# Seven quarter products for the queries of fourteen head pairs, and a layernorm spread over seven heads

## The chip, the cores and the metric

The kernel runs on one core of one Trainium2 chip. The metric is the device time of one execution in microseconds; the time of a kernel is the median of its runs. Engines are named as in the profile: PE is TensorE (matmuls; PEld are its weight loads), DVE is VectorE, ACT is ScalarE, POOL is GpSimd, SP is SyncE, which here only issues transfers.

## The reference

One transformer block with adaptive layernorm: 2 batches of 1024 tokens, 256 channels, 16 heads of 128, all float32. Queries and keys get a bias and a rotary turn, the attention is causal, and a gated feed-forward part follows.

```python
h = _layernorm(x) * (1 + ca) + sa
q = (h @ Wq + bq) * scale; k = h @ Wk + bk; v = h @ Wv + bv   # per head: (n, 128)
q = q * cos + rotate_half(q) * sin                            # k alike
attn = softmax(where(causal, -max, q @ k.T))
x = x + ga * ((attn @ v) @ Wo + bo)
h = _layernorm(x) * (1 + cb) + sb
x = x + gb * ((silu(h @ Wgate) * (h @ Wup)) @ Wdown)
```

## The kernel before

The attention is cut into 32 units, one for each batch, group of two heads, and head: `units = [(b, g, h) ...]`, numbered `n`. Even `n` is the first head of its group (h = 0), odd `n` the second (h = 1). A unit runs eight steps `i`, one for each block of 128 queries. The whole program is written inside `tc.manual_schedule()`: each engine executes its instructions in the order in which the loop at lines 879 to 927 writes them.

In step `i` that loop writes, in this order:

- `shared_out` (L629, L632): one output projection of an older head on PE into the only bank of `ps_y`, and on DVE the sum `x += py * rden`. The next output projection can't start before this sum has read the bank.
- `score` (L542, L545): the product of query block i with the keys up to it, into one of two buffers of `ps_sc`, and on DVE the masked row minimum `nmax`.
- `turned` (L576, L588): the 32x32 turn of the probabilities of step i-1 on DVE; after steps 3 and 7 it issues 16 transfers on SP that put the blocks in place (`pT`).
- `expo` (L562): the exponential on ACT.
- `release`: what `project_qk` left over from the step before (see below).
- `project_qk` (L499 to L521) in steps 1, 3, 4 and 5: half the tokens (512) of the queries or keys of the next unit.
- `values` (L603, L611): probabilities times values of the unit before, in steps 0, 6 and 7.
- products of the values (`value_step`) in steps 0, 2 and 3, and `extras`: layernorm, weights of the feed-forward part, gates.

A projection of a query half is two matmuls into one bank of `ps_a` (two banks in all), one for each half of the 256 channels. ACT then adds the bias and swaps the halves of the head into `r1` (two instructions of 64 x 512, L511, reading the bank), POOL multiplies `r1` by the sine table (L512); in `release` of the next step DVE writes `dst = (pq + bias) * cos` (L515, reading the bank and the cosine table), and POOL adds `r1` to it (L518).

The values of groups 2 to 15 (counted over both batches, 14 groups) are not computed head by head. Both heads and both token halves of a group form a 2 x 2 product of quarters (tokens half by channel half, weights channel half by head), which `value_step` (L453 to L488) does with 7 quarter products in place of 8, in Winograd's way: `token_sum` makes four sums of token quarters once per batch (`tT`), `weight_sums` (L440) makes four sums of 128 x 128 weight quarters for each group on POOL, and the products are put together by two copies on ACT (`snap`), five additions on DVE that read a bank and a `snap`, and two additions on POOL. Steps 1 to 3 are in the second head of the group before, steps 4 to 7 in the group's own first head.

The layernorms between (of batch 1 before its attention, and of batch 0 before its feed-forward part) lie in `extras` (L792 to L812): statistics of the 8 token blocks (L224, L225) in units m-5 and m-4, a square root on ACT (L229) in m-4, scaling and a 32x32 turn of each block (L240, L273) in m-3 and m-2, with m = 14 and 30. The feed-forward weights are scaled on DVE (L318) in units 6, 7 and 8, in steps 2 and 5; `add_bias` (L398) adds a row to x on POOL in every step of units 17 and 20. `gate_rows("b")` issues two row broadcasts on SP in unit 7.

Of the kernel before, what the change touches and what calls it, by code (L numbers as in the profile page):

```python
# [11 lines left out]
F32 = mybir.dt.float32  # L12
I32 = mybir.dt.int32
AF = mybir.ActivationFunctionType
ALU = mybir.AluOpType
PSUM = bass.MemoryType.PSUM

P = 128
B, S, D = 2, 1024, 256
H, DH = 16, 128  # L20
HID = 704
NT = S // P
KC = D // P
HG = 2
# [3 lines left out]
QB = 512  # L28
# [9 lines left out]
def adaln_block(ctx: ExitStack, tc: tile.TileContext, a, cos_d, sin_d, out):  # L38
    nc = tc.nc
    pool = lambda name, bufs, **k: ctx.enter_context(tc.tile_pool(name=name, bufs=bufs, **k))  # L40

    const = pool("const", 1)
# [4 lines left out]
    ps_a = pool("ps_a", 2, space=PSUM)  # L47
# [14 lines left out]
    def load_x(b, t, n, eng):  # L62
        eng.dma_start(x[b][:, t : t + n, :], x_d[b, :, t : t + n, :])
# [19 lines left out]
    def warm_up(tiles):  # L83
# [22 lines left out]

    modT = const.tile([P, 4, KC, B], F32, name="modT")
    gate = {
        (n, b): const.tile([P, D], F32, name=f"g{n}{b}") for n in ("a", "b") for b in range(B)
    }  # L110
    bo_bc = const.tile([P, D], F32, name="bo_bc")
    bvacc = const.tile([P, D], F32, name="bvacc")
# [33 lines left out]

    def gate_rows(n):

        for b in range(B):
            row = grow_d["ab".index(n), b : b + 1, :]  # L150
            nc.sync.dma_start(gate[n, b], row.to_broadcast([P, D]))
# [51 lines left out]
    wpool = pool("w", 2)  # L203
# [182 lines left out]
    gbo = {}  # L386

    def bias_row():

        pb = ps_a.tile([P, 512], F32, tag="a", name="pbias")  # L390
        nc.tensor.matmul(pb[:, :D], ones, bvacc, start=True, stop=True)
        nc.vector.tensor_tensor(bo_bc, pb[:, :D], bo_bc, ALU.add)
        for b in range(B):
            gbo[b] = const.tile([P, D], F32, name=f"gbo{b}")
            nc.gpsimd.tensor_tensor(gbo[b], gate["a", b], bo_bc, ALU.mult)

    def add_bias(b, t):
# [39 lines left out]
        }[n]  # L437
        nc.gpsimd.tensor_tensor(tT[b, n], x0, x1, ALU.subtract)

    def weight_sums(b, g, n):  # L440

        w = weights[b, g]["v"]
        a11, a12, a21, a22 = (w[:, k, ts(h, DH)] for h in range(HG) for k in range(KC))
        if n == 0:
            s2 = tpool.tile([P, DH], F32, tag="ws", name=f"ws_{b}{g}")
            wsum[b, g] = (a21, s2, a11, a12)
            nc.gpsimd.tensor_tensor(a11, a11, a21, ALU.subtract)
            nc.gpsimd.tensor_tensor(s2, a22, a11, ALU.subtract)
        else:
            nc.gpsimd.tensor_tensor(a21, a21, a22, ALU.add)  # L450
            nc.gpsimd.tensor_tensor(a12, a12, wsum[b, g][1], ALU.subtract)

    def value_step(b, g, step):  # L453
        w = weights[b, g]["v"]
        quarter = lambda k, blk: hT[b, blk][:, k, :]
        if step == 1:
            vs[b, g] = vpool.tile([P, NT, HG * DH], F32, tag="v", name=f"v_{b}{g}")
            for n in (1, 2):
                snap[n] = tpool.tile([P, QB], F32, tag=f"s{n}", name=f"snap{n}_{b}{g}")
        part = lambda h, blk: vs[b, g][:, ts(blk, QB // P), ts(h, DH)]  # L460
        tiles = lambda t: t.rearrange("p (t d) -> p t d", d=DH)

        def product(tokens, wq):
            bank = ps_a.tile([P, 512], F32, tag="a", name=f"pv{step}_{b}{g}")
            for r in range(QB // P):
                nc.tensor.matmul(bank[:, ts(r, P)], tokens[:, ts(r, P)], wq, start=True, stop=True)  # L466
            return bank

        add = lambda eng, to, x0, x1: eng.tensor_tensor(to, x0, x1, ALU.add)  # L469
        if step == 1:  # L470
            nc.scalar.copy(snap[1], product(quarter(0, 0), w[:, 0, ts(0, DH)]))
        elif step == 2:
            bank = product(quarter(1, 0), w[:, 1, ts(0, DH)])
            add(nc.vector, part(0, 0), tiles(bank), tiles(snap[1]))
        elif step == 3:
            add(nc.vector, snap[1], product(tT[b, 2], wsum[b, g][1]), snap[1])
        elif step == 4:
            bank = product(quarter(1, 1), wsum[b, g][3])
            add(nc.vector, part(0, 1), tiles(bank), tiles(snap[1]))
        elif step == 5:  # L480
            nc.scalar.copy(snap[2], product(tT[b, 1], wsum[b, g][0]))  # L481
            add(nc.gpsimd, part(0, 1), part(0, 1), tiles(snap[2]))
        elif step == 6:
            add(nc.vector, snap[1], product(tT[b, 3], wsum[b, g][2]), snap[1])
            add(nc.gpsimd, part(1, 1), tiles(snap[1]), tiles(snap[2]))
        else:
            bank = product(tT[b, 4], w[:, 1, ts(1, DH)])
            add(nc.vector, part(1, 0), tiles(bank), tiles(snap[1]))  # L488

    def project_qk(u, s, n):  # L490

        b, g, h = u
        head = g * HG + h
        if n == 0:
            qks[u, s] = qkpool.tile([P, S], F32, tag=f"{s}T", name=f"{s}T_{b}{g}{h}")
        dst = qks[u, s]
        pq = ps_a.tile([P, 512], F32, tag="a", name=f"p{s}_{b}{g}{h}{n}")
        for k in range(KC):
            nc.tensor.matmul(  # L499
                pq,  # L500
                weights[b, g][s][:, k, ts(h, DH)],
                hT[b, n][:, k, :],
                start=(k == 0),
                stop=(k == KC - 1),
            )
        c = (R_BQ if s == "q" else R_BK) + head
        sl, half = ts(n, QB), DH // 2

        r1 = rot.tile([P, QB], F32, tag="r1", name=f"r1_{s}{b}{g}{h}{n}")
        for to, of in ((slice(0, half), slice(half, DH)), (slice(half, DH), slice(0, half))):  # L510
            nc.scalar.activation(r1[to], pq[of], AF.Identity, bias=cols[of, c : c + 1])  # L511
        nc.gpsimd.tensor_tensor(r1, r1, sin_t[:, sl], ALU.mult)  # L512

        def rest():
            nc.vector.scalar_tensor_tensor(  # L515
                dst[:, sl], pq, cols[:, c : c + 1], cos_t[:, sl], ALU.add, ALU.mult
            )
            nc.gpsimd.tensor_tensor(dst[:, sl], dst[:, sl], r1, ALU.add)  # L518


        held.append(rest)  # L521
# [234 lines left out]
    def extras(n, i):  # L756
# [8 lines left out]
            gate_b()  # L765
        if n == 6 and i == 3:
            gate_b_turn()
        if n == 7 and i == 3:
            gate_rows("b")

        if n in (2, 15) and i in (0, 1, 3):
            for m in {0: (1, 2), 1: (3,), 3: (4,)}[i]:
                token_sum(n // 15, m)
        if n > 2 and n % 2 and i in (0, 3) and n + 1 < N:
            weight_sums(*units[n + 1][:2], i // 3)

        if n == 2 and i == 7:
            ffn_scale_load()
        for m, name in ((5, "gate"), (6, "up"), (7, "last")):
            if n == m and i == 7:  # L780
                ffn_weight_load(name)
            if n == m + 1 and i in (2, 5):
                ffn_weight_scale(name, i // 4)
        if n in (3, 4, 8, 9) and i == 7:
            load_x(1, {3: 0, 4: 2, 8: 4, 9: 6}[n], 2, nc.scalar)
        if n == 29 and i == 7:
            ffn_down_load()
        if n == 31 and i in (1, 3, 5):
# [2 lines left out]

        for m, b, name in ((14, 1, "a"), (30, 0, "b")):  # L792

            j = i - 1 if n in (m - 5, m - 3) else i + 3
            if n in (m - 5, m - 4) and 1 <= i <= 4:
                ln_stats(b, name, j)
            if n == m - 4 and i == 6:
                ln_sqrt(b, name, 0, NT)
            if n in (m - 3, m - 2) and 2 <= i <= 5:
                ln_move(b, name, j - 1)  # L800
            if n in (m - 3, m - 2) and 1 <= i <= 4:
                ln_scale(b, name, j // 4, (j % 4,))
            if n in (m - 2, m - 1) and i == 6:
                ln_send(b, name, ((0, 1), (2, 3))[n - m + 2])
            if n == m and i in (4, 5, 7):
                blk = i // 6
                if i != 5:
                    dest = (new_hT if b else new_h2)(b, blk)
                else:
                    dest = (hT if b else h2s)[b, blk]  # L810
                for f in {4: (0,), 5: (1,), 7: (0, 1)}[i]:
                    ln_shift(b, name, blk, 0 if b else 2, dest, f)  # L812
# [4 lines left out]
        if n == 20:  # L817
            add_bias(1, i)

    filler = (0, 1, 3, 4, 5, 6)  # L820

    def shared_out(s, late=False):
# [3 lines left out]
    with tc.manual_schedule():  # L826
# [52 lines left out]
        for n, u in enumerate(units):  # L879
# [5 lines left out]
            for i in range(NT):  # L885
# [2 lines left out]
                if owed:  # L888
                    owed.pop()()
                ps, nmax = score(u, i)  # L890
                if n > 2 and h == 0 and i == 3:
                    value_step(b, g, 7)
                if i >= 1:
                    turned(u, i - 1)
                elif prev:
                    turned(prev, NT - 1)
                expo(u, i, ps, nmax)
                release()
                if i in (1, 3, 4, 5) and nxt:
                    project_qk(nxt, *{1: ("q", 0), 3: ("k", 0), 4: ("q", 1), 5: ("k", 1)}[i])  # L900
                if i in (6, 7) and prev:
                    values(prev, 1, 4 * (i - 6), 4 * (i - 5))

                if i in (0, 2):
                    if n in (1, 2):
# [1 line left out]
                            project_v(0, 1, 2 + 2 * n)  # L907
                    elif n == 0:
                        project_v(b, n, 4 + i, ps_o, "o")

                if n > 2 and (h == 0 or more) and i in (0, 2):
                    vg = (nb, ng) if h else (b, g)
                    for step in {(1, 0): (1, 2), (1, 2): (3,), (0, 0): (4, 5), (0, 2): (6,)}[h, i]:
                        value_step(*vg, step)
                if n == 0 and i in (6, 7):
                    project_v(0, 1, 2 * (i - 6))
                if not nxt and i in filler:
# [1 line left out]

                if prev and i == (0 if n > 2 else 2):  # L920
                    values(prev, 0, 0, 4)
                extras(n, i)
                if i == 7 and h == 1:
                    if more:
# [125 lines left out]
```

## Time and profile before

| | |
|---|---|
| median of 3 runs | 1061.25 us (1060.69 to 1061.36) |
| the profiled execution | 1061.52 us, of which the profile spans 1059.7 us |
| granted TensorE clock | 1.000 |
| busy: DVE, ACT, POOL | 701.0, 491.3, 468.5 us |
| transfers | 132.34 MB, 125 GB/s on average |

The share of busy time is over the whole span; a unit of the attention lasts 28.5 to 29.5 us in the middle of it, and in it PE's work follows without a gap. The span and what lies around it (1.82 us) make up the profiled execution's time.

### The profile page before, as it was taken

Reading aid. Unit: us, or ns where it says so; the run is one execution under the profiler, and the core shown is the slowest. Engines: PE = TensorE matmul, PEld = TensorE weight load, DVE = VectorE, ACT = ScalarE, POOL = GpSimd, SP = SyncE. Lnnn points to the kernel's source line nnn. Section 1 sums busy time; section 2 is a strip of 40 time slices with the busy share of each in tenths; the row PEclk is TensorE's granted clock in tenths of the full one; section 3 lists DMA queues with packets and bytes.
Section 4 is the critical chain, followed back from the end, with each engine's and each line's share of the span. In section 5 each row is a group of like instructions: output and inputs, shape, how many; then the busy total and the mean of one; then the engine's idle time right before and its main releaser. Section 6 shows DMA issues by size and latency. Waiting matters only on the chain.

```text
span 1059.7 us, 13263 instructions
## 1 busy us (share of the span) xinstructions
PE 1055.0 (100%) x3834; PEld 638.4 (60%) x3834; DVE 701.0 (66%) x1523; ACT 491.3 (46%) x930; POOL 468.5 (44%) x461
## 2 busy tenths in 40 slices
PE   9999999999999999999999999999999999999998
PEld 5655566566666665665666666666565666555747
DVE  5667776777777776766676666666777866545331
ACT  5644444454445454444554444454454554562110
POOL 5755464645353554855644544434444544200100
PEclk9999999999999999999999999999999999999999
DMA  5466646666565646565565656454555657423201
GB/s 191 91 173 161 155 112 153 148 148 150 125 157 117 147 112 155 112 152 120 117 148 113 147 113 152 107 144 97 144 112 128 144 132 171 107 59 71 70 0 40
DMA packets 68379, 132.34 MB, mean 125 GB/s; under 512 B 19366, under 2 KB 23476, under 8 KB 68308
## 3 DMA queue, kind: packets, MB, share of 16 engines
q1 hardware_dynamic: 66060, 126.17, 50.6%
q10 hardware_dynamic: 2168, 5.20, 1.5%
q8 instruction: 31, 0.51, 0.2%
q14 instruction: 40, 0.33, 0.1%
q0 software_dynamic: 80, 0.13, 0.1%
HBM read 25.52 MB, written 2.10 MB: 26 GB/s over the span
## 4 chain that ended last, share of the span: by engine, by line
PE 99%; DVE 0%; issue 0%; POOL 0%; POOLq 0%
PE po L603 23%; PE ps L542 23%; PE py L629 10%; PE pq L499 10%; PE pk L499 10%; PE pv L466 8%; PE pgu L658 7%; PE pd L716 2%; PE pv L411 1%; PE pd_0w L716 1%; PE pd_1w L716 1%; PE warm_ps L85 0%; PE ptx_a L254 0%; PE pd L705 0%; PE pm L122 0%; DVE wupT L318 0%
## 5 line engine op out<-in xcount | busy, mean ns | idle before, releaser
L562 ACT ACTIVATE p<-ps,nmax 128x128 f32<-128x128 f32 (+7 forms) x256 | 190.3, 743 | 353.9 <-DVE nmax L545 353.6
L542 PE MATMUL ps<-kT,qT 128*128 128x512 f32 (+3 forms) x768 | 289.6, 486 | 0.0
L603 PE MATMUL po<-pT,v 128*128 128x512 f32 (+3 forms) x768 | 263.7, 486 | 0.2 <-DMA pT<-t 0.2
L545 DVE CUSTOM_DVE_ANT_0 ps<-ps,mask 128x128 f32<-128x128 f32 (+7 forms) x256 | 195.1, 762 | 100.5 <-PE ps L542 100.1
L632 DVE SCALAR_TENSOR_TENSOR x<-py,rden,x 128x256 f32<-128x256 f32 x256 | 122.2, 479 | 179.7 <-PE py L629 176.3
L603 PEld LDWEIGHTS po<-pT,v 128*128 128x128 f32 x768 | 143.6, 190 | 122.5 <-issue 93.5
L576 DVE STREAM_TRANSPOSE t<-p 128x128 f32<-128x128 f32 (+7 forms) x256 | 197.9, 773 | 5.3 <-DMA pT<-t 3.0
L542 PEld LDWEIGHTS ps<-kT,qT 128*128 128x128 f32 x768 | 145.8, 190 | 77.4 <-issue 63.4
L512 POOL TENSOR_TENSOR r_q<-r_q,sin_t 128x512 f32<-128x512 f32 x64 | 82.4, 1287 | 162.4 <-ACT r_q L511 161.0
L629 PE MATMUL py<-wo,o 128*128 128x256 f32 x512 | 151.8, 381 | 0.3 <-DVE x L632 0.3
L629 PEld LDWEIGHTS py<-wo,o 128*128 128x128 f32 x512 | 90.0, 191 | 77.5 <-issue 49.1
L499 PE MATMUL pq<-hT,wq 128*128 128x512 f32 x256 | 120.5, 593 | 0.0
L499 PE MATMUL pk<-hT,wk 128*128 128x512 f32 x256 | 120.3, 592 | 0.0
L512 POOL TENSOR_TENSOR r_k<-r_k,sin_t 128x512 f32<-128x512 f32 x64 | 81.7, 1277 | 47.0 <-ACT r_k L511 46.8
L518 POOL TENSOR_TENSOR kT<-kT,r_k 128x512 f32<-128x512 f32 x64 | 81.2, 1269 | 42.2 <-DVE kT L515 36.4
L511 ACT ACTIVATE r_q<-pq,cols 64x512 f32<-64x512 f32 x128 | 87.6, 684 | 23.5 <-PE pq L499 19.9
L518 POOL TENSOR_TENSOR qT<-qT,r_q 128x512 f32<-128x512 f32 x64 | 81.8, 1278 | 27.1 <-DVE qT L515 24.6
L511 ACT ACTIVATE r_k<-pk,cols 64x512 f32<-64x512 f32 x128 | 87.6, 684 | 10.7 <-PE pk L499 7.0
L499 PEld LDWEIGHTS pk<-hT,wk 128*128 128x128 f32 x256 | 47.5, 190 | 41.4 <-issue 34.9
L499 PEld LDWEIGHTS pq<-hT,wq 128*128 128x128 f32 x256 | 46.1, 190 | 32.8 <-issue 30.3
L611 ACT COPY o<-po 128x512 f32<-128x512 f32 x64 | 37.3, 582 | 59.5 <-PE po L603 59.5
L469 POOL TENSOR_TENSOR v<-v,snap 128x512 f32<-128x512 f32 x14 | 17.7, 1265 | 93.2 <-ACT snap L481 93.2
(135 smaller groups left out, 967.5 us busy)
## 6 DMA issues: line engine op xcount, KB each, us to landing
pT<-t SPq DMA_DIRECT2D x512, 128.0 KB, 2.4
pT<-t SPq DMA_DIRECT2D x512, 64.0 KB, 2.0
wq<-in_Wq SPq DMA_DIRECT2D x16, 256.0 KB, 3.1
wk<-in_Wk SPq DMA_DIRECT2D x16, 256.0 KB, 4.1
wv<-in_Wv SPq DMA_DIRECT2D x16, 256.0 KB, 4.1
wo<-in_Wo SPq DMA_DIRECT2D x16, 256.0 KB, 3.0
out<-yo SPq DMA_DIRECT2D x15, 128.0 KB, 1.7
x<-in_x ACTq DMA_DIRECT2D x4, 256.0 KB, 3.1
```

Source lines behind the costliest of these rows:

```text
L466: nc.tensor.matmul(bank[:, ts(r, P)], tokens[:, ts(r, P)], wq, start=True, stop=True)
L499: nc.tensor.matmul(pq, weights[b, g][s][:, k, ts(h, DH)], hT[b, n][:, k, :], start=(k == 0), stop=(k == KC - 1),)
L511: nc.scalar.activation(r1[to], pq[of], AF.Identity, bias=cols[of, c : c + 1])
L512: nc.gpsimd.tensor_tensor(r1, r1, sin_t[:, sl], ALU.mult)
L518: nc.gpsimd.tensor_tensor(dst[:, sl], dst[:, sl], r1, ALU.add)
L542: nc.tensor.matmul(ps[:, c:e], qT[:, ts(i, P)], kT[:, c:e], start=True, stop=True)
L545: nc.vector.tensor_tensor_reduce(ps[:, :L], ps[:, :L], mask[:, NT - 1 - i :, :].rearrange("p t k -> p (t k)"), -SCALE, FLT_MAX, ALU.add, A ...
L562: nc.scalar.activation(p[:, :L], ps[:, :L], AF.Exp, bias=nmax, scale=-1.0, accum_out=dens[u][:, i : i + 1])
L576: nc.vector.transpose(t32[blk][:, :, j, : i + 1, :].rearrange("p c k b -> p k c b"), p[:, : (i + 1) * P].rearrange("p (k c a) -> p k c a", ...
L603: nc.tensor.matmul(po[:, off * P :], vs[b, g][:, k, ts(h, DH)], pT[:, off:, :, k, :], start=(k == 0), stop=(k == last),)
L629: nc.tensor.matmul(py[:, :D], outs[u][:, ts(t, P)], weights[b, g]["o"][:, h, :], start=True, stop=True)
L632: nc.vector.scalar_tensor_tensor(x[b][:, t, :], py[:, :D], rdens[u][:, t : t + 1], x[b][:, t, :], ALU.mult, ALU.add)
```

## The change

The queries of the same 14 groups are now made by the same 7 quarter products. `value_step` becomes `set_step(b, g, name, step)` and serves both; for the queries a product is one matmul with 512 columns in which the weight quarter is the stationary operand. The two heads' queries of the next group are made in the second head of a group (h = 1), the values of a group in its own first head (h = 0), one product in each of seven steps. `project_qk` is left for the keys (from unit 3 on), in steps 3 and 5 of h = 1 and in steps 2 and 5 of h = 0.

A finished quarter of the queries is in SBUF, no longer in a bank: `rotary` (which holds what followed the matmuls in `project_qk`) reads it there, and its last two operations write it in place. `rotary` is called from the list `due`, after the `values` of the same step. `weight_sums` makes the sums for queries too, in steps 0 and 1 of the same unit, in a new order.

```diff
-    def value_step(b, g, step):
-        w = weights[b, g]["v"]
+    due = []
+
+    def set_step(b, g, name, step):
+        w = weights[b, g][name]
...
+        if name == "q" and step in (1, 6):
+            h = step // 6
+            qks[(b, g, h), "q"] = qkpool.tile([P, S], F32, tag="qT", name=f"qT_{b}{g}{h}", bufs=3)
...
+                nc.tensor.matmul(bank, wq, tokens, start=True, stop=True)
             return bank
 
+        def done(h, blk):
+            if name == "q":
+                due.append(lambda: rotary((b, g, h), "q", blk, part(h, blk)))
...
         elif step == 2:
             bank = product(quarter(1, 0), w[:, 1, ts(0, DH)])
             add(nc.vector, part(0, 0), tiles(bank), tiles(snap[1]))
+            done(0, 0)
         elif step == 3:
-            add(nc.vector, snap[1], product(tT[b, 2], wsum[b, g][1]), snap[1])
+            nc.scalar.copy(snap[2], product(tT[b, 1], s1))
         elif step == 4:
-            bank = product(quarter(1, 1), wsum[b, g][3])
+            add(nc.vector, snap[1], product(tT[b, 2], s2), snap[1])
+        elif step == 5:
+            bank = product(quarter(1, 1), s4)
             add(nc.vector, part(0, 1), tiles(bank), tiles(snap[1]))
-        elif step == 5:
-            nc.scalar.copy(snap[2], product(tT[b, 1], wsum[b, g][0]))
             add(nc.gpsimd, part(0, 1), part(0, 1), tiles(snap[2]))
+            done(0, 1)
         elif step == 6:
-            add(nc.vector, snap[1], product(tT[b, 3], wsum[b, g][2]), snap[1])
+            add(nc.vector, snap[1], product(tT[b, 3], s3), snap[1])
             add(nc.gpsimd, part(1, 1), tiles(snap[1]), tiles(snap[2]))
+            done(1, 1)
         else:
             bank = product(tT[b, 4], w[:, 1, ts(1, DH)])
             add(nc.vector, part(1, 0), tiles(bank), tiles(snap[1]))
+            done(1, 0)
...
+    STEPS = (
+        {0: 1, 1: 2, 3: 3, 4: 4, 5: 5, 6: 6, 7: 7},
+        {0: 1, 1: 2, 2: 3, 4: 4, 5: 5, 6: 6, 7: 7},
+    )
...
-                if i in (1, 3, 4, 5) and nxt:
-                    project_qk(nxt, *{1: ("q", 0), 3: ("k", 0), 4: ("q", 1), 5: ("k", 1)}[i])
+                setted = n > 2 and (not h or more) and ((nb, ng, "q") if h else (b, g, "v"))
+                if setted and i in STEPS[h]:
+                    set_step(*setted, STEPS[h][i])
+                if n < 3:
+                    proj = {1: ("q", 0), 3: ("k", 0), 4: ("q", 1), 5: ("k", 1)}
+                else:
+                    proj = {3 if h else 2: ("k", 0), 5: ("k", 1)}
+                if i in proj and nxt:
+                    project_qk(nxt, *proj[i])
                 if i in (6, 7) and prev:
                     values(prev, 1, 4 * (i - 6), 4 * (i - 5))
+                while due:
+                    due.pop(0)()
```

The layernorms in `extras` take seven units: statistics of two blocks in each of units m-8 to m-5 (steps 1 and 2), the square root in m-5, and scaling and turn of three blocks in each of m-4 to m-2 (steps 1 to 4).

```diff
-            j = i - 1 if n in (m - 5, m - 3) else i + 3
-            if n in (m - 5, m - 4) and 1 <= i <= 4:
-                ln_stats(b, name, j)
-            if n == m - 4 and i == 6:
+            if m - 9 < n < m - 4 and i in (1, 2):
+                ln_stats(b, name, 2 * (n - m + 8) + i - 1)
+            if n == m - 5 and i == 3:
                 ln_sqrt(b, name, 0, NT)
-            if n in (m - 3, m - 2) and 2 <= i <= 5:
-                ln_move(b, name, j - 1)
-            if n in (m - 3, m - 2) and 1 <= i <= 4:
-                ln_scale(b, name, j // 4, (j % 4,))
+            t = 3 * (n - m + 4) + i - 1
+            if m - 4 <= n < m - 1 and 2 <= i <= 4 and t - 1 < NT:
+                ln_move(b, name, t - 1)
+            if m - 4 <= n < m - 1 and 1 <= i <= 3 and t < NT:
+                ln_scale(b, name, t // 4, (t % 4,))
```

To make room for a third query buffer, the two gate rows of the feed-forward part lie in a weight buffer and are loaded in unit 30 rather than in unit 7, the two rows of `gbo` overwrite `bvacc` and `bo_bc`, and two loads of x for batch 1 are issued a unit or two earlier.

## The prediction

> **What bounds the kernel now.** I read the page's busy shares first, then the chain that ended last, then the groups of PE by shape, and at the end the timelines of single units.
>
> ```profile
> PE 1055.0 (100%) x3834; PEld 638.4 (60%) x3834; DVE 701.0 (66%) x1523; ACT 491.3 (46%) x930; POOL 468.5 (44%) x461
> ...
> PE 99%; DVE 0%; issue 0%; POOL 0%; POOLq 0%
> ```
>
> PE works for 1055.0 of the 1059.7 us and makes up 99% of the chain. Its waits sum to 1.6 us: 1.1 at the start, 0.33 for a sum of L632 (unit 7) and 0.2 for a `pT` transfer. So each us of PE work that goes is a us of the end, as long as no other engine makes PE wait. How long an instruction holds PE is read from starts that follow each other, since the recorded lengths overlap:
>
> ```profile
> 160.39 1.88 PE L499 MATMUL pq<-hT,wq 128*128 128x512 f32 x4
> 162.11 0.59 PE L629 MATMUL py<-wo,o 128*128 128x256 f32 x2
> 162.54 0.81 PE L542 MATMUL ps<-kT,qT 128*128 128x384 f32 x2
> 163.19 1.05 PE L466 MATMUL pv<-ws,tT 128*128 128x128 f32 x8
> 164.08 0.60 PE L629 MATMUL py<-wo,o 128*128 128x256 f32 x2
> 164.51 1.02 PE L542 MATMUL ps<-kT,qT 128*128 128x512 f32 x2
> ```
>
> A matmul shows as two instructions. A query half (two matmuls of 512 columns) holds PE for 162.11 - 160.39 = 1.72 us; one 512-column score holds it 0.86 us (the next row starts at 165.37); a quarter product of the values, made of four 128-column matmuls, 0.89 us; an output projection 0.43 us.
>
> The engines behind PE, in a plain odd unit (5) and one with layernorm (11); columns are PE, PEld, DVE, ACT, POOL:
>
> ```profile
> 155.36:183.86 28.50, 28.50 (x105) 17.25 (x104) 19.66 (x44) 13.70 (x28) 11.79 (x12) 1.00 0.60 141
> 328.00:356.60 28.60, 28.60 (x105) 17.24 (x104) 22.42 (x53) 14.88 (x28) 11.84 (x12) 1.00 0.50 111
> ```
>
> DVE is the second: 19.66 of 28.50 us, before the change adds to it.
>
> **The change on PE.** Per group, 8 matmuls of 512 columns for the queries become 7: 4 x 1.72 = 6.88 us become 7 x 0.86 = 6.02 us. 14 x 0.86 = 12.0 us go. That a product which stands alone costs no more than half a pair is read from the single score above. The rest of PE's list keeps its instructions. Per unit the work moves little: an odd unit swaps three value products (2.67) and 3.44 of queries for 6.02, an even one four value products and 3.44 for seven (6.23); both come to about 28.5 us.
>
> **What is added elsewhere, 14 times each.** ACT: two copies of 128x512 at 0.58 (L471, L481), 16 us in all, and four rotary pairs (L511, 1.37 each) that now read SBUF. The only bound I have for another source is the ACT rows of this width, 0.58 to 0.78 us, so -0.1 to +0.1 each; ACT is busy for half a unit, which hides it. POOL: two additions at 1.27 to 1.32 (L469) and four weight sums at 0.455 (L447), 62 us in all. DVE: five additions at 0.60 from start to start (the L469 rows record 0.677), 42 us in all. An odd unit, which now holds all queries, goes on DVE from 19.66 by two more L515 (0.63 start to start) and three more additions to 22.7 us, and on POOL to 12 x 1.27 + 2 x 1.27 + 4 x 0.455 = 19.6 us, both of 28.4. On rates alone all of this hides under PE.
>
> **The new cost: a DVE turn with both operands in SBUF.** Before, L515 read a bank and the cosine table. A query quarter is now in SBUF, so 56 of the L515 read two SBUF operands. The trace has that form in L318, beside POOL's additions:
>
> ```profile
> 193.68 1.27 POOL L518 TENSOR_TENSOR qT<-qT,r_q 128x512 f32<-128x512 f32 x1
> 193.96 1.67 DVE L318 SCALAR_TENSOR_TENSOR wgateT<-raw,s_bc 128x640 f32<-128x640 int32 x1
> 194.91 1.85 POOL L469 TENSOR_TENSOR v<-snap,snap 128x512 f32<-128x512 f32 x1
> 204.02 0.81 DVE L318 SCALAR_TENSOR_TENSOR wgateT<-raw,s_bc 128x640 f32<-128x640 int32 x1
> 204.08 1.88 POOL L512 TENSOR_TENSOR r_q<-r_q,sin_t 128x512 f32<-128x512 f32 x1
> ```
>
> The same DVE instruction takes 0.81 us when it starts before POOL's, and 1.67 when POOL began 0.28 us earlier: it ends 0.7 us after POOL's does. The POOL instruction that comes second takes 1.85 or 1.88 in place of 1.27. So the later one waits for the other's whole instruction. A query turn costs 0.63 if it comes first, up to 0.63 + 1.27 if not.
>
> The Trainium skill speaks against the change here: "SBUF — State Buffer", section "Who interferes with whom", says that a DVE instruction with two SBUF inputs and a GpSimd one that reads SBUF exclude each other for a whole instruction. By it all 56 turns could lose up to a POOL instruction; the rows above agree, and the sum below doesn't rest on the page.
>
> Does that wait reach PE? The tight spot is `ps_y`'s only bank: output projection i+1 waits for DVE's sum of step i, which stands behind all DVE work of step i-1. Take t = 0 at the end of query product 2 (step 1 of an odd unit). PE: projection 0.43, score 1.08, product 3 1.94, projection 2.37, score 3.23, key half 4.95; then projection 4 wants the sum of step 3. DVE: addition until 0.8, sum 1.25, minimum (0.48) 1.75, turn of the probabilities (0.37) 2.1. ACT makes `r1` (1.38) from 0.8 to 2.2; then POOL's sine product (1.27) runs from 2.3 to 3.55, and DVE's query turn, which overwrites what ACT reads, is free at 2.2 too. If DVE comes first it ends at 2.85 and the sum of step 3 at 3.3: 1.65 us to spare. If POOL does, 4.2 and 4.65: 0.3 to spare. The last quarter (product 7, turned in step 0 of the next unit) leaves 0.9 us by the same count, or nothing where POOL is first, as it probably is, for DVE arrives 0.4 us after ACT is done.
>
> What eats these margins, with POOL first: unit 7, two blocks of statistics (0.5 each from start to start) and a weight scaling of 0.74 to 1.67, of which one block hides in the wait: 1.8 us. Units 6 and 8, the same in an even unit: 1.0 each. Units 11 and 27, scale and turn of two blocks (0.55 and 0.36 each): 0.6 each. Units 9, 23 and 25, statistics: 0.2 each. Unit 17, where POOL has eight `add_bias` of 0.73 more and ACT and DVE wait behind it: 0.8. The other groups 0.15 each, 2.0. Sum 8.4 us. With DVE first nearly all of it is covered: 0.5. The traced pairs give no rule for a tie; since POOL leads at the last quarter of every group and POOL's list is dense in step 6, I take two thirds, 5.5 us.
>
> **Edits that I cost at nothing.** The layernorms keep their instructions; spread, they take an even load from units 12, 13, 28 and 29 and put it in short steps, which is in the list above. The square root and its two table loads (1.28 each) move to unit 9, step 3; by the count above the exponential of step 4 then ends at 11.3, and score 6 wants its buffer at 12.0; uncovered, 2 us. The gate rows take 1.08 us of SP in unit 7 and lie in a gap (SP idle from 226.8 to 228.9 before the next 16 transfers); in unit 30 they are at the same step, and what queues behind them is the first half of `pT`; uncovered, 1.1 us once. `gbo` in place and the earlier loads of x keep their instructions.
>
> **The sum.** 1059.7 - 12.0 + 5.5 = 1053.2 of span, with the 1.82 us around it 1055.0; the profiled execution was 0.27 us above the median, so 1054.7 us.
>
> **The rivals.**
> 1. *All waits hide* (DVE first in most ties, or POOL's waits shorter): 0.5 us of stalls, 1061.25 - 12.0 + 0.5 = 1049.8. For it: PE waited 0.33 us in unit 7 before, although DVE there ran L318 for 1.67 us in the same step. Against it: the slots after products 2 and 3 are shorter now (step 1 of an odd unit 1.72 us of PE, before 2.58).
> 2. *DVE becomes the pacer of odd units*, which ends on the slower side. The query turn must wait not for one POOL instruction but for two in a row, since POOL has the next one ready. Half the turns at 2.54 and half at 1.27 make 22.7 + 7.6 = 30.3 us of DVE in a unit of 28.4: 1.9 x 14 = 26.6, 1075.8 us. It decides from 28.4 - 22.7 + 0.86 = 6.6 us of such waits per odd unit, 1.64 per turn; all four at two would give 63 us. For it: POOL's sine products and additions stand back to back in steps 5 and 6. Against it: in the two rows of 1.67 us DVE's wait was 0.86 us and the POOL instruction behind was held, so a waiting DVE is let in.
> 3. *The gain is eaten*: stalls between 9.9 and 14.1 us, the bound of 8.4 above plus what I cost at nothing; about 1061. For it: my count has no time for signals between engines (POOL starts L512 0.08 us after ACT's L511 ends).
> 4. *A lone product costs more than half a pair*: were it 0.05 us, 98 x 0.05 = 4.9 us less gain, 1059.6 with the forecast's stalls. Only the single score speaks, and against it.
>
> **How the numbers follow.** Forecast (1 to 9.9 us of stalls, rival 4 within it) 0.50; rival 1 0.27; rival 3 0.08; rival 2 0.15. The likeliest gives 1054.7, its own range 1050.2 to 1059.1. Reaching to rival 1 and over rival 3, and leaving out rival 2 and the tail below, the range is 1049.3 to 1063.0. No change means within 0.2% (2.1 us), about what a measurement can tell: rival 3 alone, 0.08; faster 0.77; slower 0.15.
>
> **What would show it.** Right: 98 lone query products, each holding PE 0.86 us; PE's busy time down by 12; L515 on queries in odd units at a mean between 0.7 and 2.0 us; PE's waits for L632 of 1 to 9 us, longest in unit 7. Wrong: waits of PE for anything but L632, such as a weight sum on POOL or a bank of `ps_a`; DVE above 28 us in plain odd units; or no waits at all.

## The result, and the profile after

The changed kernel takes 1066.66 us (median of 5 runs, 1065.90 to 1068.35), the kernel before 1061.36 us beside it (5 runs, 1060.69 to 1063.03). The ratio is 1.005, 95% interval 1.0035 to 1.0065: slower by 0.5%, where the forecast was 0.6% faster. The profiled execution took 1067.2 us and spans 1065.4 us, at a granted clock of 1.000.

The busy shares and the chain of the changed kernel:

```profile
PE 1050.1 (99%) x3806; PEld 633.1 (59%) x3806; DVE 779.6 (73%) x1593; ACT 505.8 (47%) x958; POOL 540.7 (51%) x545
...
PE 80%; DVE 13%; issue 2%; POOL 1%; DMA 1%; ACT 1%; SPq 1%; DVEq 0%; ACTq 0%; POOLq 0%
PE ps L579 20%; PE po L640 18%; PE py L666 9%; PE pk L529 8%; PE pgu L695 7%; PE pv L483 6%; PE pq L487 6%; DVE qT L552 4%; DVE t L613 2%; DVE ps L582 2%; PE pd L753 2%; DVE qT L494 1%; PE pq L529 1%; DVE x L669 1%; PE pv L416 1%
```

PE has the 28 matmul instructions less, yet only 80% of the chain is PE, where it was 99%: DVE is now 13% of it, with the query turn (L552) as its largest line. DVE's busy time rose by 78.6 us. PE's recorded busy time fell by 4.9 us only, though 12.0 us of work are gone from its list: a matmul that is held is recorded longer (0.70 us for 0.59 in the last row of the passage below), so about 7 us of what PE loses stand inside its busy time.

PE's waits (us in total, times, longest):

```profile
PE py L666 <- DVE x L669: 9.1, 17, 1.1
PE pv L483 <- DVE v L494: 1.3, 1, 1.3
PE warm_ps L85 <- POOL ones L79: 1.1, 1, 1.1
```

The wait is the one that the prediction named, for the sum that frees the bank of `ps_y`. The view counts a wait only past the recorded end of the instruction before, and records of matmuls overlap, so it understates the loss. I therefore took the gap between the starts of each two successive matmul instructions and subtracted the median gap of the width of the earlier one (0.429 us for 512 columns, 0.3225 for 384, 0.216 for 256, 0.112 for 128). What is left over, where it is more than 0.01 us and summed over the span ("stalls" from here on), is 6.4 us before and 24.1 us after. The change saves 12.0 us of PE and adds 17.7 us of stalls: +5.7, which is the difference of the spans (1065.4 - 1059.7). Stalls are always those of the one profiled execution, which can lie up to 2.5 us from the median of its kernel's runs.

That the saving is there is seen in unit 19, in PE's timeline (start, length):

```profile
576.69 1.02 PE L487 MATMUL pq<-tT,wsq 128*128 128x512 f32 x2
577.55 0.59 PE L666 MATMUL py<-wo,o 128*128 128x256 f32 x2
577.98 1.45 PE L579 MATMUL ps<-kT,qT 128*128 128x512 f32 x4
579.27 1.02 PE L487 MATMUL pq<-hT,wq 128*128 128x512 f32 x2
580.13 1.88 PE L529 MATMUL pk<-hT,wk 128*128 128x512 f32 x4
```

A lone product holds PE from 576.69 to 577.55, and another from 579.27 to 580.13: 0.86 us each, half a pair.

Units 19 (odd) and 20 (even), which have no layernorm and no weights of the feed-forward part (start and end; length; busy time of PE, PEld, DVE, ACT, POOL; clock; DMA share; GB/s):

```profile
565.27:593.67 28.40, 28.40 (x87) 15.66 (x86) 22.25 (x43) 15.70 (x31) 16.34 (x15) 1.00 0.62 148
593.67:622.78 29.11, 28.91 (x130) 19.38 (x129) 22.11 (x44) 12.85 (x27) 19.97 (x24) 1.00 0.49 109
```

No engine is near its limit: DVE works 22.25 of 28.40 us. A plain group takes 28.40 + 29.11 = 57.51 us where, by the starts of its scores, it took 28.50 + 29.39 = 57.89: of the 0.86 us that left PE's list 0.48 comes back, as one stall in the even unit.

The query turns and what stands before them (busy us, mean ns of one, idle before):

```profile
L552 DVE SCALAR_TENSOR_TENSOR qT<-qT,cols,cos_t 128x512 f32<-128x512 f32 x56 | 87.9, 1570 | 4.7 <-ACT r_q L548 4.3
L552 DVE SCALAR_TENSOR_TENSOR kT<-pk,cols,cos_t 128x512 f32<-128x512 f32 x64 | 45.4, 710 | 0.8 <-ACT r_k L548 0.8
L548 ACT ACTIVATE r_q<-qT,cols 64x512 f32<-64x512 f32 x112 | 80.6, 719 | 88.4 <-POOL qT L494 67.0
```

The same line takes 710 ns on keys, which it reads from a bank, and 1570 ns on queries, which it reads from SBUF. 87.9 - 56 x 0.71 = 48 us of DVE are waiting inside the instruction.

The place where PE pays, at the end of unit 19 and the start of unit 20 (the timeline, with rows left out; in brackets the idle time before and what ended it):

```profile
590.87 1.45 ACT L548 ACTIVATE r_q<-qT,cols 64x512 f32<-64x512 f32 x2 [4.46 <-POOL qT L494]
...
592.47 1.27 POOL L549 TENSOR_TENSOR r_q<-r_q,sin_t 128x512 f32<-128x512 f32 x1 [1.63 <-ACT r_q L548]
592.60 1.68 DVE L552 SCALAR_TENSOR_TENSOR qT<-qT,cols,cos_t 128x512 f32<-128x512 f32 x1
594.21 0.68 DVE L494 TENSOR_TENSOR qT<-pq,snapq 128x512 f32<-128x512 f32 x1
594.81 0.47 DVE L669 SCALAR_TENSOR_TENSOR x<-py,rden,x 128x256 f32<-128x256 f32 x1
594.98 1.45 ACT L548 ACTIVATE r_q<-qT,cols 64x512 f32<-64x512 f32 x2 [0.95 <-DVE qT L494]
595.41 1.23 DVE L613 STREAM_TRANSPOSE t<-p 128x1024 f32<-128x1024 f32 x1
596.51 1.27 POOL L549 TENSOR_TENSOR r_q<-r_q,sin_t 128x512 f32<-128x512 f32 x1 [0.81 <-ACT r_q L548]
596.57 1.76 DVE L552 SCALAR_TENSOR_TENSOR qT<-qT,cols,cos_t 128x512 f32<-128x512 f32 x1
598.52 0.48 DVE L669 SCALAR_TENSOR_TENSOR x<-py,rden,x 128x256 f32<-128x256 f32 x1
599.07 0.70 PE L666 MATMUL py<-wo,o 128*128 128x256 f32 x2 [0.20 <-DVE x L669]
```

Two quarters are turned in one passage. POOL multiplies product 6's quarter by the sine from 592.47; DVE's turn of the same quarter, which starts at 592.60, ends at 594.28, 0.54 us after POOL's instruction has. So DVE adds up product 7 only at 594.21, ACT reads the sum from 594.98, and now the second meeting comes: POOL at 596.51, DVE at 596.57, 1.76 us long. Behind it stands the sum of L669 (598.52), and behind that PE's projection at 599.07.

### The profile page after: what moved, and what is told of

It reads as the page before. It is cut to its first block, busy times and chain, and to the rows that moved or that the text cites. A ratio compares the mean times of both kernels' runs of the same rounds, so it can differ in the third digit from the quotient of the medians.

```text
span 1065.4 us, 13531 instructions
## 1 busy us (share of the span) xinstructions
PE 1050.1 (99%) x3806; PEld 633.1 (59%) x3806; DVE 779.6 (73%) x1593; ACT 505.8 (47%) x958; POOL 540.7 (51%) x545
## 4 chain that ended last, share of the span: by engine, by line
PE 80%; DVE 13%; issue 2%; POOL 1%; DMA 1%; ACT 1%; SPq 1%; DVEq 0%; ACTq 0%; POOLq 0%
PE ps L579 20%; PE po L640 18%; PE py L666 9%; PE pk L529 8%; PE pgu L695 7%; PE pv L483 6%; PE pq L487 6%; DVE qT L552 4%; DVE t L613 2%; DVE ps L582 2%; PE pd L753 2%; DVE qT L494 1%; PE pq L529 1%; DVE x L669 1%; PE pv L416 1%
## 5 line engine op out<-in xcount | busy, mean ns | idle before, releaser
L669 DVE SCALAR_TENSOR_TENSOR x<-py,rden,x 128x256 f32<-128x256 f32 x256 | 121.6, 476 | 113.9 <-PE py L666 108.7
L666 PE MATMUL py<-wo,o 128*128 128x256 f32 x512 | 154.5, 386 | 9.5 <-DVE x L669 9.1
L666 PEld LDWEIGHTS py<-wo,o 128*128 128x128 f32 x512 | 87.8, 190 | 86.1 <-issue 42.6
L548 ACT ACTIVATE r_q<-qT,cols 64x512 f32<-64x512 f32 x112 | 80.6, 719 | 88.4 <-POOL qT L494 67.0
L555 POOL TENSOR_TENSOR kT<-kT,r_k 128x512 f32<-128x512 f32 x64 | 86.6, 1353 | 29.0 <-DVE kT L552 27.5
L548 ACT ACTIVATE r_k<-pk,cols 64x512 f32<-64x512 f32 x128 | 87.3, 682 | 11.6 <-PE pk L529 8.1
L552 DVE SCALAR_TENSOR_TENSOR qT<-qT,cols,cos_t 128x512 f32<-128x512 f32 x56 | 87.9, 1570 | 4.7 <-ACT r_q L548 4.3
L290 POOL TENSOR_SCALAR h<-xt_b,modT 128x512 f32<-128x512 f32 x8 | 6.3, 798 | 96.6 <-DMA xt_b<-t 96.6
L483 PEld LDWEIGHTS pv<-wv,tT 128*128 128x128 f32 x336 | 44.0, 191 | 18.7 <-issue 13.4
```

What stands on the lines that cost most here:

```text
L552: nc.vector.scalar_tensor_tensor(dst[:, sl], pq, cols[:, c : c + 1], cos_t[:, sl], ALU.add, ALU.mult)
L666: nc.tensor.matmul(py[:, :D], outs[u][:, ts(t, P)], weights[b, g]["o"][:, h, :], start=True, stop=True)
L669: nc.vector.scalar_tensor_tensor(x[b][:, t, :], py[:, :D], rdens[u][:, t : t + 1], x[b][:, t, :], ALU.mult, ALU.add)
```

## The experiments

In the expectations, P is the theory that the query turn's meeting with POOL's sine product is the cause: both read SBUF, and the end of ACT's pair lets both go. N puts the time down to the layernorms spread over more units, W to DVE's added work, the five additions per group. The ratios are against the kernel before, run on the same chip; its median there was 1061.65 to 1062.37 us.

**1. The changed kernel with the old place of the layernorms** (e1). The lines of `extras` as they were:

```diff
-            if m - 9 < n < m - 4 and i in (1, 2):
-                ln_stats(b, name, 2 * (n - m + 8) + i - 1)
...
+            j = i - 1 if n in (m - 5, m - 3) else i + 3
+            if n in (m - 5, m - 4) and 1 <= i <= 4:
+                ln_stats(b, name, j)
...
```

> The queries by quarter products, with the layernorms as before the change (statistics in units m-5 and m-4, scaling and turns in m-3 and m-2). Theory P (the query turns that read two SBUF operands wait on DVE for POOL, and DVE's sum of L669 then comes late for PE): the layernorm matters little, 1064 to 1069 us, the 56 query turns keep their mean of 1.5 to 1.6 us. Rival N (the spread layernorm in the short steps 1 and 2 is what makes PE wait): under 1062 us.

1067.74 us, ratio 1.0057 (1.0045 to 1.0069); stalls 23.1 us, query turns 1.585 us on average. The loss stays without the spread.

**2. The kernel before with only the spread** (e2): the same lines the other way round, and the two earlier loads of x.

> The kernel before, with only the layernorms spread over seven heads (and the two earlier loads of x that this needs). Theory P: 1060.5 to 1062.5 us, PE waits for L632 under 2 us. Rival N: 1064 us or more.

1061.86 us, ratio 1.0001 (0.9993 to 1.001); stalls 6.1 us. The spread is worth nothing to PE before the change and nothing after it; N is out.

**3. Two of the four quarters stay in the bank** (e3). Products 2 and 7 get their addition in place in PSUM, and `rotary` reads the bank; the number and order of instructions are as in the changed kernel.

```diff
         elif step == 2:
             bank = product(quarter(1, 0), w[:, 1, ts(0, DH)])
-            add(nc.vector, part(0, 0), tiles(bank), tiles(snap[1]))
-            done(0, 0)
+            to = bank if name == "q" else part(0, 0)
+            add(nc.vector, to, tiles(bank), tiles(snap[1]))
+            done(0, 0, to)
...
-            add(nc.vector, part(1, 0), tiles(bank), tiles(snap[1]))
-            done(1, 0)
+            to = bank if name == "q" else part(1, 0)
+            add(nc.vector, to, tiles(bank), tiles(snap[1]))
+            done(1, 0, to)
```

> The changed kernel, but products 2 and 7 of the queries get their snap added in place in their PSUM bank, and the rotary part reads the bank, as it did before the change. The DVE additions stay, 28 of the 56 turns have one SBUF operand again. Theory P: these 28 turns take 0.70 to 0.75 us in place of 1.75 to 1.86, DVE's busy time falls by 25 to 32 us, PE's waits in step 2 of even units (10.5 us now) fall below 4, and the time is 1054 to 1060 us. Rival W (the five more additions per group on DVE, in shorter steps, are what makes DVE late): 1065 to 1067 us, with the waits still there.

1054.71 us (1053.31 to 1057.96), ratio 0.9937 (0.9923 to 0.9951): 12 us below the changed kernel. Its turns, by where they read:

```profile
L554 DVE SCALAR_TENSOR_TENSOR qT<-qT,cols,cos_t 128x512 f32<-128x512 f32 x28 | 35.9, 1282 | 1.1 <-ACT r_q L550 1.0
L554 DVE SCALAR_TENSOR_TENSOR qT<-pq,cols,cos_t 128x512 f32<-128x512 f32 x36 | 26.0, 721 | 3.6 <-ACT r_q L550 3.6
```

and the same passage of its timeline:

```profile
588.98 0.68 DVE L494 TENSOR_TENSOR pq<-pq,snapq 128x512 f32<-128x512 f32 x1
...
589.76 1.38 ACT L550 ACTIVATE r_q<-pq,cols 64x512 f32<-64x512 f32 x2 [0.96 <-DVE pq L494]
...
591.21 1.28 POOL L551 TENSOR_TENSOR r_q<-r_q,sin_t 128x512 f32<-128x512 f32 x1 [0.75 <-ACT r_q L550]
591.34 0.70 DVE L554 SCALAR_TENSOR_TENSOR qT<-pq,cols,cos_t 128x512 f32<-128x512 f32 x1
...
592.35 0.48 DVE L671 SCALAR_TENSOR_TENSOR x<-py,rden,x 128x256 f32<-128x256 f32 x1 [0.21 <-PE py L668]
```

POOL's instruction runs as before and DVE's turn lies wholly inside it, at 0.70 us; the sum now waits for PE, no longer PE for the sum. All of DVE's additions are still there, so W is out. Stalls are 14.1 us, in an execution of 1057.20 us, 2.5 above the median. A plain even unit takes 28.64 us, not 29.11.

**4. The two-input form alone** (e4). In the kernel before, ACT copies the query bank to SBUF and DVE's turn reads the copy; ACT's pair still reads the bank, so that DVE needn't wait for it.

```diff
+        src = pq
+        if s == "q" and (b, g) > (0, 1):
+            src = dst[:, sl]
+            nc.scalar.copy(src, pq)
...
-                dst[:, sl], pq, cols[:, c : c + 1], cos_t[:, sl], ALU.add, ALU.mult
+                dst[:, sl], src, cols[:, c : c + 1], cos_t[:, sl], ALU.add, ALU.mult
```

> The kernel before, but the queries of groups 2 to 15 are copied by ACT from the bank into their SBUF tile and DVE's turn reads them there; products, additions and layernorms as before. It adds the two-SBUF turn (56 times) and 56 ACT copies of 0.58, and no other work. Theory P: these turns take a mean of 1.2 to 1.9 us, PE waits for L632 2 to 10 us, 1063 to 1071 us. Rival W: 1061 to 1062.5 us.

1060.70 us, ratio 0.9994 (0.9985 to 1.0002): P's expectation missed. The turns have two SBUF operands, and in 46 of 56 cases they cost what they cost from the bank (0.71 us):

```profile
L519 DVE SCALAR_TENSOR_TENSOR qT<-qT,cols,cos_t 128x512 f32<-128x512 f32 x56 | 45.0, 804 | 0.0
```

The timeline of unit 5 says why:

```profile
163.98 0.71 DVE L519 SCALAR_TENSOR_TENSOR qT<-qT,cols,cos_t 128x512 f32<-128x512 f32 x1
...
164.12 1.70 POOL L516 TENSOR_TENSOR r_q<-r_q,sin_t 128x512 f32<-128x512 f32 x1 [6.67 <-ACT r_q L515]
```

DVE doesn't wait for ACT here (idle before: 0.0) and is 0.14 us ahead of POOL, so it is POOL that waits: 1.70 in place of 1.27 us, on an engine with time to spare. The other ten turns, which take 0.79 to 1.78 us, all begin 0.03 to 1.04 us after a POOL instruction that they overlap, and end 0.55 us after it. So the form is a cost where DVE comes second, and here it seldom does.

**5. The form with the wait** (e9). As before, but ACT's pair reads the copy too, so that DVE's turn, which overwrites the copy, has to wait for ACT. One operand differs from e4:

```diff
-            nc.scalar.activation(r1[to], pq[of], AF.Identity, bias=cols[of, c : c + 1])
+            nc.scalar.activation(r1[to], src[of], AF.Identity, bias=cols[of, c : c + 1])
```

> The kernel before with the SBUF copy of the queries of groups 2 to 15 (as in the run in which the turn read the copy and took 0.80 us), and now ACT's rotary pair reads the copy too, so that DVE's turn overwrites what ACT reads and must wait for it, as in the changed kernel. Theory P in its present form (the meeting is made by the place: DVE and POOL are let go by the same end of ACT's pair): the turns rise clearly above 0.80, to a mean of 1.0 to 1.7 us, and DVE's busy time by 10 us or more; PE's list has the wider slots of the kernel before, so the time moves by 0 to 6 us, 1061 to 1067 us. Rival (the changed kernel's turns are long for another reason, such as its denser POOL list): the mean stays under 0.9 us and the time at 1061.

1083.02 us, ratio 1.02 (1.0186 to 1.0215): 22 us above e4, more than expected. The turns:

```profile
L519 DVE SCALAR_TENSOR_TENSOR qT<-qT,cols,cos_t 128x512 f32<-128x512 f32 x56 | 79.2, 1414 | 6.7 <-ACT r_q L515 6.7
```

and one meeting, from the timeline:

```profile
493.66 1.26 POOL L516 TENSOR_TENSOR r_q<-r_q,sin_t 128x512 f32<-128x512 f32 x1 [5.02 <-ACT r_q L515]
493.68 1.78 DVE L519 SCALAR_TENSOR_TENSOR qT<-qT,cols,cos_t 128x512 f32<-128x512 f32 x1 [0.23 <-ACT r_q L515]
...
496.12 1.12 PE L499 MATMUL pk<-hT,wk 128*128 128x512 f32 x2 [0.56 <-DVE snap L469]
```

This kernel has no product saved and no addition more. The copies alone cost nothing (e4 spans 1058.9 us); with the one operand changed as well, 20.6 us of span are lost against the kernel before (1080.3 against 1059.7), and its stalls are 27.0 us, also 20.6 more. DVE's idle time before the turns is 6.7 us in all, where the turns themselves are 34.2 us longer than in e4, so most of the delay is the meeting with POOL and not the wait for ACT. Of the stalls 11.6 us stand before the key half of even units, which needs a bank of `ps_a` that a late addition (L469) holds, and 10.0 before the projection of step 4 in odd units: a late DVE made PE wait at two banks, not at `ps_y` alone.

**6. All four quarters in the bank** (e5). POOL adds the two snaps once, and DVE adds the result to the banks of products 5 and 6 in place (one addition more per group on DVE, one less on POOL); product 6 goes after the values of its step.

```diff
+            if name == "q":
+                add(nc.gpsimd, part(1, 1), snap[1], snap[2])
         elif step == 5:
             bank = product(quarter(1, 1), s4)
+            if name == "q":
+                add(nc.vector, bank, bank, part(1, 1))
+                done(0, 1, bank)
...
         elif step == 6:
...
+            if name == "q":
+                add(nc.vector, bank, bank, part(1, 1))
+                done(1, 1, bank)
```

> All four finished query quarters stay in their bank: POOL adds the two snaps once into a free query tile, DVE adds that sum to the banks of products 5 and 6 in place (one more DVE addition, one POOL addition less per group), product 6 stands after the values of step 6. No query turn reads two SBUF operands and ACT no longer waits for a POOL addition. Theory P: all 56 turns at 0.70 to 0.75 us, PE's waits below those of the two-quarter version (14.1 us by gaps between starts, of which 6.4 stood in the kernel before), 1051 to 1056 us. Rival W (DVE additions): slower than the two-quarter version's 1054.7, since DVE gets 14 additions more.

1055.50 us (1054.75 to 1057.36), ratio 0.9944 (0.9931 to 0.9956); stalls 11.3 us. All turns are short now:

```profile
L563 DVE SCALAR_TENSOR_TENSOR qT<-pq,cols,cos_t 128x512 f32<-128x512 f32 x64 | 46.3, 723 | 3.8 <-ACT r_q L559 3.8
```

It is no better than e3: the intervals overlap. The two quarters that e3 leaves in SBUF meet POOL (product 6, 1.68 us in a plain unit) or miss it (product 5, 0.74), and in the plain units no stall follows from either.

**7. The same with the old place of the layernorms** (e7; the edits of e5 and e1).

> All quarters in their bank, with the layernorms as before the change. Theory P: DVE has room again, so the layernorm's place is worth under 2 us either way against the same kernel with the spread one. Rival N: 3 us or more slower than with the spread layernorm.

1055.42 us, ratio 0.9944 (0.9932 to 0.9957), as e5: the spread is worth nothing in the repaired kernel either.

**8. Half of the layernorm's transfers issued by ACT** (e8, on top of e5), for the stalls that e3 has left in units 14 and 30 (in e5's own profile they are 0 and 0.7 us).

```diff
-                ln_send(b, name, ((0, 1), (2, 3))[n - m + 2])
+                ln_send(b, name, ((0, 1), (2, 3))[n - m + 2], eng=(nc.sync, nc.scalar)[n - m + 2])
```

> All quarters in their bank, and the second half of the layernorm's transfers (units 13 and 29, step 6) issued by ACT instead of SP. In the two-quarter version units 14 and 30 lose 1.6 and 1.4 us, DVE's turn of step 4 there waiting for the probabilities' transfers behind them on SP. Theory: 1 to 3 us faster than all quarters in their bank alone. Rival (the transfers themselves are late, whoever issues them): no difference.

1060.97 us, ratio 0.9995 (0.9987 to 1.0004): 5.5 us above e5, which no theory had expected. ACT's timeline in unit 13:

```profile
408.47 0.64 ACTq L287 DMA_DIRECT2D xt_a<-xt_a  x1
...
409.15 6.15 ACTq L287 DMA_DIRECT2D xt_a<-xt_a  x7
415.35 1.11 ACT L610 ACTIVATE p<-ps,nmax 128x1024 f32<-128x1024 f32 x1 [5.63 <-DMA xt_a<-xt_a]
```

Eight issues hold ACT's queue for 6.8 us, 0.85 us each, and the exponential stands behind them. Unit 14 stalls for 5.4 us, unit 30 for 2.9.

**9. Order only: the last quarter's turn one step later** (e6). In the changed kernel the held turn isn't let go in steps 0 and 1 of an even unit, where POOL has finished when it comes.

```diff
-                release()
+                if not (n > 3 and h == 0 and i < 2):
+                    release()
```

> The changed kernel with one edit of order: in even units nothing is released in steps 0 and 1, so that the turn of the last query quarter (made by product 7) and its POOL addition are issued in step 2. It still reads two SBUF operands and no work is taken away. Theory P in the form 'the cost is the meeting with POOL, not the form' (the SBUF turn that did not meet POOL took 0.80 us): this quarter's 14 turns fall from 1.76 to about 0.75, PE's wait in step 2 of even units from 10.5 to under 5 us, 1058 to 1063 us. Rival form 'two SBUF operands are slow wherever they stand': the turns stay at 1.7 and the waits move to step 3, 1064 to 1068 us.

1062.32 us, ratio 1.0005 (0.9996 to 1.0014): 4.3 us below the changed kernel. The last quarter's turns take 0.71 us, the others are as they were, and the stall before the projection of step 2 in even units (10.5 us in the changed kernel) is gone. Stalls are 21.2 us, of which 3.9 are in unit 2, in front of a product that waits for `pT`; the edit doesn't reach that unit.

**10. Order only: the first quarter's turn held too** (e10):

```diff
-                if not (n > 3 and h == 0 and i < 2):
+                if not (n > 3 and h == 0 and i < 2) and not (n > 2 and h == 1 and i == 2):
                     release()
```

> The changed kernel with order edits alone: in even units nothing is released in steps 0 and 1, and in odd units nothing in step 2, so that the turns of the first and of the last query quarter stand a step or two later, when POOL's sine product is done. Work, operands and banks as in the changed kernel. Theory P: both quarters' turns at 0.75 in place of 1.75 to 1.86 (DVE's busy time 28 us below the changed kernel's 779.6), PE's waits in step 3 of odd units (4.2 us) fall below 2, 1056 to 1061 us. Rival (what helped in the version with two quarters in their bank was the bank, or ACT reading PSUM): 1061 us or more.

1060.69 us, ratio 0.9984 (0.9976 to 0.9993); the profiled execution, 1058.74 us with stalls of 15.6, was the lowest of eleven. The turns:

```profile
L552 DVE SCALAR_TENSOR_TENSOR qT<-qT,cols,cos_t 128x512 f32<-128x512 f32 x56 | 56.5, 1009 | 1.4 <-ACT r_q L548 1.1
```

Of the 4.2 us before the projection of step 4 in odd units 0.5 are left, but 2.9 are now before that of step 5: a held turn is moved work, and what it is moved to can be late too. DVE's busy time fell by 20.6 us (to 759.0), where 28 were expected. Theory and rival meet at 1061 us, so the time alone doesn't decide between them; the turns do. Moving the meeting apart helps, taking it away (e3, e5) helps more: e10 spares the same two quarters as e3 and its median is 6 us higher, which wasn't explained.

## Why the prediction was wrong

**PE's list: right.** 98 lone products at 0.86 us, 12.0 us less; with that number the saving and the stalls add up to the difference of the spans. Rival 4 (a lone product that costs more) falls with it.

**The engines' rates: right.** POOL's and DVE's added work hides under PE. DVE's 22.25 us in an odd unit have the waits in them, where the count gave 22.7 without; but the turn and the addition of the last quarter, which the count put into the odd unit, fall into the even one (594.21 and 596.57, after 593.67).

**The new cost was named rightly, and its price per turn lay within the bounds given** (0.63 to 1.90 from start to start; recorded 0.73 to 1.87). The Trainium skill's "SBUF — State Buffer", section "Who interferes with whom", has the rule behind it, and e4 against e9 agrees with its sentence "Issue order, not op shape, decides who blocks.": the same shapes, 0.80 and 1.41 us on average. The recorded starts don't give that order where they lie within 0.05 us of each other (see the last section).

**The step that failed is "Does that wait reach PE?", in its term "The other groups 0.15 each, 2.0."** The sum took 5.5 us of stalls, 8.4 at most; 17.7 came. In units 3 to 30 the stalls stand against the list like this (us):

| units | predicted with POOL first | measured |
|---|---|---|
| 7 | 1.8 | 1.5 |
| 6 and 8 | 2.0 | 1.5 |
| 11 and 27 | 1.2 | 2.5 |
| 9, 23 and 25 | 0.6 | 1.4 |
| 17 | 0.8 | 0 |
| all others | 2.0 | 12.6 |
| sum | 8.4 | 19.5 |

In these units the kernel before had 1.0 us. The units that the list singled out for their other work came to 6.9 us against 6.4. Of the 12.6 us in all other units, 2.3 are in the five plain even ones (0.46 to 0.47 each), 7.4 in units 4, 10, 18, 26 and 30 (1.2 to 2.0 each), which the list lacks, and 2.9 in units 3, 5, 12 and 28. By place, 10.5 of the 19.5 us stand before the projection of step 2 in even units, behind the last quarter's turn: 0.45 or more in each of the 14.

- *The count at the last quarter had one meeting, and there are two.* It gave nothing to spare with POOL first, reckoned from product 7 on. But the addition of product 7 stands behind the turn of product 6's quarter, which had itself waited for POOL (592.60 to 594.28). A plain even unit so has -0.47 us to spare. e3 and e6 show that the second meeting is needed for this stall: with the last turn away from POOL it goes. That the first one is needed too is counted from the timeline (that turn is 1.68 us in place of 0.71); no run takes away the first alone.
- *The passage itself starts late in some units.* Product 5's turn passes POOL at 0.73 to 0.80 us in nine odd units, but in units 7, 9, 11, 25 and 27 it meets it too and takes 1.24, 1.50, 1.13, 1.48 and 1.12 us. Product 6's addition on POOL then comes later, and before the projection of step 2 the units behind (8, 10, 12, 26, 28) stall for 0.97, 1.07, 0.85, 1.07 and 0.85 us in place of 0.46. Unit 17's `add_bias`, for which the list had 0.8 us in unit 17, delays the same addition on POOL by 0.7 us, and its price is found in unit 18 (1.05 us at the same place, 0.6 above a plain unit).
- *The tie.* "I take two thirds" was wrong in the same direction: in the three quarters that meet the sine product, POOL was first 42 times of 42. In 16 of them DVE sat idle until ACT's pair ended, so that one event let both go, and POOL won each time; in the other 26 DVE was still at earlier work and came 0.06 to 0.14 us after POOL. So it isn't a matter of chance in this kernel. With POOL first throughout the sum would have been 8.4 of stalls and 1057.6 us, still on the wrong side, so the count at the last quarter weighs more than the tie.

**The rivals.** Rival 2 had the side but not the mechanism: DVE is no pacer, and the wait per turn is 0.86 us (1.570 - 0.710), for one POOL instruction, well below its deciding 1.64. The loss comes from where the wait stands, in front of the one sum that frees `ps_y`, with DVE idle for a fifth of the unit. Rival 3 had the size nearest (stalls of 9.9 to 14.1) and was passed. Rival 1 fell. Of the signs of being wrong that the prediction named, one appeared, and it is small: a wait for something other than the sum, 1.3 us for an addition of the values (L494) in unit 30.

**Edits costed at nothing.** The spread of the layernorms: right as a sum (e1, e2, e7), though it moves stalls: of unit 30's 2.0 us 1.5 are a wait for L494, which e1 doesn't have; e1 loses 1.8 and 1.6 us in units 12 and 28 instead, against 0.85 each. Since e1 has the gate rows where the changed kernel has them, that wait isn't theirs alone.

**What is left open.** With the meeting gone, e3 and e5 still have 7.7 and 4.9 us more stalls than the kernel before. 1.9 of each stand before the key half of odd units, which waits for a bank that a query quarter holds longer; the rest lies in single units (2, 6, 14, 26, 30), partly behind `pT` transfers, and differs between the two kernels, each of which was profiled once (e3 2.5 us above its median, e5 0.75 below). It wasn't settled.

## What to carry to other kernels

Before an operand is moved from PSUM to SBUF, look at who else is let go by the same instruction: here two readers released at once, on DVE with two SBUF inputs and on POOL, ran one after the other (1.86 us for DVE in place of 0.71), and the loser's delay counted where a bank that PE needs again waited behind it. A margin near such a bank has to be counted through all such meetings in the passage, not from the last event on. The remedy here was to leave one operand in the bank: adding in place in PSUM made this change worth 0.6% (0.9937 and 0.9944), with the same products.

## What the runs showed of the hardware that was not expected

- *A recorded start isn't a grant.* In 16 meetings of the changed kernel DVE's turn is recorded 0.04 to 0.05 us ahead of POOL's sine product, and still ends 0.55 us after it; in the other 26 of the 42 POOL is 0.06 to 0.14 us ahead. In e4 a lead of 0.14 us was enough for DVE to run in 0.71 us. At which lead between these the order turns wasn't measured.
- *The loser's tail.* The turn that waited ends 0.55 us after POOL's instruction in nearly all of them (median 0.548), where 0.71 is its whole length alone, so most of its own work comes after POOL's end. The ten long turns of e4 end 0.55 us after POOL's instruction too.
- *Issuing transfers from ACT* cost 0.85 us each there, eight in a row (e8), and the exponential behind them waited 5.63 us.
